# Layer 0's output turned by VectorE and DRAM instead of TensorE, with instruction orders for three engines

## The chip, the core and the metric

The kernel runs on one NeuronCore of a Trainium2 chip. The metric is the device time of one execution in microseconds (us), the median of several runs. A profile of one more execution shows when each instruction ran on the five engines: TensorE (PE in the profile; its weight loads are PEld), VectorE (DVE), ScalarE (ACT), GpSimd (POOL) and SyncE (SP), which here only issues DMA transfers. Each engine works through its own instructions in a fixed order and waits at an instruction whose inputs or buffers are not ready.

## What is computed

The input x has 128 batches of 64 nodes with 256 features. Four graph layers follow each other, each in the form `x = layernorm(x + layer(x))`. The change concerns layers 0 and 1, which the kernel runs in one fused stage:

```python
# layer 0: dense attention over the 64 nodes of a batch
Wh = einsum('bnf,fo->bno', h, W)
e = (Wh @ a1)[:, :, None] + (Wh @ a2)[:, None, :]
e = where(e >= 0, e, 0.2 * e);  e = where(adj == 0, -inf, e)
out = einsum('bij,bjo->bio', softmax(e), Wh)
# layer 1: attention over 512 edges, 4 heads
Xq, Xv = H @ W_lin.T, H @ W_val.T
e = einsum('behd,hd->beh', leaky_relu(Xq[:, src] + Xq[:, dst], 0.2), a) + log(A0[src, dst] + eps)
attn = segment_softmax(e, src)
out = segment_sum(attn[..., None] * Xv[:, dst], src) @ W_out.T
```

Layer 2 (two matrix products with batch norms) and layer 3 (two graph convolutions and four small LSTMs) come after it and are not touched.

## The kernel before

**Quarters.** The fused stage cuts the input into 16 quarters q of 512 rows, that is 8 batches; a batch is called a graph b, 0 to 7. All work is in 32-bit floats. A quarter lives in a tile of 128 partitions by 1024 numbers, `A[:, q]`; before its layer-0 result arrives there, that place is free and serves as scratch.

**Steps of layer 0**, by function: `l0_a` makes the transposed input x^T. For q = 0 TensorE does it (eight 128x128 transposes, ScalarE copies them out). For q ≥ 1 the DMA brings x in "squares": `load_x` issues eight transfers of 64 KB (L135) that put each 32x32 block where it belongs in the transposed layout, and one VectorE instruction (L220, `nc.vector.transpose`) turns every block in itself. `l0_b` multiplies with W (L230) and ScalarE copies the results out; `l0_c` builds the attention logits (transposes L241, VectorE L244 to L248, ScalarE exponentials L251); `l0_d` transposes the attention (L260); `l0_e` multiplies it with Wh (L270), adds x on VectorE (L273), takes mean and variance (L92, L93, L82, L95) and normalises on GpSimd: a power (L83) and four multiply-adds (L97). The result x1 of the quarter goes to `A[:, q]`.

**Steps of layer 1.** `l1_t` transposes x1 on TensorE (L204, eight matmuls) with two ScalarE copies (L205). `l1_qv(q, c2)` makes half of a quarter's queries and values (L295, L298; ScalarE L305, VectorE L306 for the queries' two parts); it is called twice per quarter. `l1_graph(q, b)` is one graph: two matmuls into `z` (L332) and a ScalarE ReLU `u` (L334). `sums` reduces four graphs over the heads (L323). Once for two quarters, in the even quarters, the softmax over edges runs: `l1_softmax` (matmul L342, VectorE scans L344 to L351, ScalarE exponential L352), `l1_sums` (two scans, L357 and L358), `l1_weights` (transposes L366, VectorE L372 and L374, four indirect DMAs to a DRAM table L378 on GpSimd, two loads `ld` from it, L384 on SP). `v_a` copies a quarter's attention out of `ld` on GpSimd (L391) and multiplies it with the values (L399, ScalarE copies L403); `v_b` multiplies with W_out (L413), adds x1 (L415), normalises on VectorE and GpSimd (L97 again, on `y`) and stores the result; `v_c` applies layer 2's adjacency (L433, ScalarE L437).

**Order.** Quarter q's loop runs its eight graphs, and behind each graph the steps of a table `between[b]`, which belong to neighbouring quarters: layer 0 is two quarters ahead, `v_a` three behind (LAG), `v_b` and `v_c` four. The first quarters therefore have no `v` steps and the last two no layer-0 steps. The program is recorded in this order and a scheduler then places every instruction in its engine's queue. `step` ties each step with `tc.issue_after` to the last instruction of the step before; only TensorE's instructions are tied this way. On the other engines the scheduler chose the order. It also chose which of the three PSUM banks named `m` each product takes; a product can only start when the bank's last reader is done.

```python
            if queue:
                with tc.issue_after(queue[-1]):
                    do(n, *more)
            else:
                do(n, *more)
            mine = [t for t in traced[first:] if t.engine == mybir.EngineType.PE]
            queue.extend(mine[-1:])
```

All the transfers of SP go through one queue, in order: loads of x and its squares, the stores of layer 1's result (L418) and the table loads.

## Time and profile before

| | |
|---|---|
| median of 3 runs | 2137.66 us (2136.54 to 2138.21) |
| the profiled execution | 2138.25 us |
| its span in the profile | 2136.4 us |
| TensorE busy | 2060.7 us, 96% of the span |
| ScalarE, VectorE, GpSimd busy | 932.1, 885.9, 430.1 us |
| fused stage (layers 0 and 1) | 0 to about 523 us |
| mean TensorE clock granted | 0.987 |

The profile is read in three steps: which engine is busy nearly all the time and where it is not (busy times by stretch), what it waits for at those places (the timeline with the releaser of each gap), and what the releaser itself was doing before (its own timeline). Busy times of matmuls overlap a little, since they are pipelined; the chain of work that ended last gives lengths without the overlap. The chain lies on TensorE for 86% of the span.

### The profile page before, as it was taken

How to read it: one execution, taken by the hardware profiler on the slowest of the kernel's cores; microseconds unless marked ns; L12 is line 12 of the kernel's file. 1: busy time of each engine (PE TensorE's matmuls, PEld its weight loads, DVE VectorE, ACT ScalarE, POOL GpSimd, SP SyncE). 2: the span in 40 equal slices, each digit the busy share in tenths (PEclk: the TensorE clock that was granted, in tenths of full speed). 3: DMA queues.
4: the chain of work that ended last, by engine and by line, in shares of the span. 5: the costliest groups of instructions: out<-in, count | busy, mean ns of one | idle time of the engine just before them, and what ended most of it. 6: DMA issues, size and time to landing. Idle time of an engine off the chain costs nothing.

```text
span 2136.4 us, 29441 instructions
## 1 busy us (share of the span) xinstructions
PE 2060.7 (96%) x11343; PEld 1330.1 (62%) x11343; DVE 885.9 (41%) x2069; ACT 932.1 (44%) x1795; POOL 430.1 (20%) x569
## 2 busy tenths in 40 slices
PE   5999999998999989999999999999999999999998
PEld 4666767665544444585576576577467468468467
DVE  7456566654444343333234334324324324323213
ACT  2776666664339014334234334334334334333333
POOL 1134334332210010121112112113103103102012
PEclk8999999998999989999999999999999999999999
DMA  5244532322240021012112102103103102101001
GB/s 144 63 69 73 85 61 53 52 43 43 43 118 29 0 89 60 21 54 66 40 46 74 40 29 90 40 11 99 50 6 104 50 1 89 50 1 60 20 1 60
DMA packets 232636, 113.41 MB, mean 53 GB/s; under 512 B 150192, under 2 KB 215728, under 8 KB 232240
## 3 DMA queue, kind: packets, MB, share of 16 engines
q1 hardware_dynamic: 230640, 109.57, 20.2%
q8 instruction: 89, 1.46, 0.3%
q0 software_dynamic: 1024, 1.05, 0.2%
q10 hardware_dynamic: 832, 0.92, 0.1%
q14 instruction: 51, 0.42, 0.1%
HBM read 67.45 MB, written 44.04 MB: 52 GB/s over the span
## 4 chain that ended last, share of the span: by engine, by line
PE 86%; DVE 6%; ACT 4%; issue 2%; POOL 1%; DMA 1%; SPq 0%; POOLq 0%; DVEq 0%; ACTq 0%
PE l L994 36%; PE l L1000 20%; PE pz L784 5%; PE pz L719 5%; PE e L323 3%; PE g L933 2%; PE g L945 2%; PE m L295 2%; PE m L230 2%; PE z L332 2%; PE m L298 2%; PE g L878 1%; PE m L413 1%; PE m L270 1%; ACT u L334 1%
## 5 line engine op out<-in xcount | busy, mean ns | idle before, releaser
L994 PE MATMUL l<-H,wih 128*128 128x256 f32 (+2 forms) x2496 | 787.5, 470 | 1.8 <-ACT H L957 1.2
L994 PEld LDWEIGHTS l<-H,wih 128*128 128x128 f32 x2496 | 471.4, 190 | 286.2 <-issue 185.6
L1000 PE MATMUL l<-hid,whh 128*128 128x256 f32 (+2 forms) x1536 | 435.9, 437 | 0.0
L1000 PEld LDWEIGHTS l<-hid,whh 128*128 128x128 f32 x1536 | 291.8, 190 | 128.4 <-issue 61.2
L1006 ACT ACTIVATE gate_i<-l,bias 128x256 f32<-128x256 f32 (+2 forms) x176 | 100.3, 570 | 441.9 <-PE l L1000 374.2
L1010 POOL TENSOR_TENSOR cell<-gate_f,cell 128x256 f32<-128x256 f32 (+2 forms) x96 | 85.0, 885 | 726.0 <-ACT gate_f L1006 726.0
L1009 DVE TENSOR_TENSOR gate_i<-gate_i,gate_g 128x256 f32<-128x256 f32 (+2 forms) x96 | 49.6, 517 | 415.1 <-ACT gate_g L1006 415.0
L83 POOL TENSOR_TENSOR ln_rs<-ln_rs,mhalf 128x2 f32<-128x2 f32 (+2 forms) x97 | 82.0, 846 | 571.6 <-DVE ln_rs L95 570.7
L334 ACT ACTIVATE u<-z 128x1024 f32<-128x1024 f32 x128 | 130.3, 1025 | 63.3 <-PE z L332 62.3
L1006 ACT ACTIVATE gate_g<-l,bias 128x256 f32<-128x256 f32 (+2 forms) x176 | 100.3, 570 | 107.9 <-PE l L994 59.5
L1014 ACT ACTIVATE gate_g<-cell 128x256 f32<-128x256 f32 (+2 forms) x176 | 90.0, 511 | 86.9 <-DVE cell L1013 45.0
L1013 DVE TENSOR_TENSOR cell<-gate_i,gate_g 128x512 f32<-128x512 f32 (+2 forms) x80 | 48.2, 602 | 186.5 <-ACT gate_g L1006 186.4
L1006 ACT ACTIVATE gate_o<-l,bias 128x256 f32<-128x256 f32 (+2 forms) x176 | 99.3, 564 | 59.9 <-PE l L1000 54.0
L719 PE MATMUL pz<-A,w 128*128 128x512 f32 x256 | 113.1, 595 | 0.0
L332 PE MATMUL z<-gath_r,qs 128*128 128x512 f32 x256 | 100.4, 480 | 0.7 <-ACT u L334 0.4
L306 DVE TENSOR_TENSOR qs<-m,qs 64x256 fp32r<-64x256 f32 x128 | 54.0, 422 | 107.0 <-ACT qs L305 104.8
L719 PEld LDWEIGHTS pz<-A,w 128*128 128x128 f32 x256 | 47.9, 190 | 55.3 <-issue 53.3
L295 PE MATMUL m<-wq,tT 128*128 128x260 f32 x256 | 71.8, 403 | 7.8 <-ACT yT L403 5.4
L1006 ACT ACTIVATE gate_f<-l,bias 128x256 f32<-128x256 f32 (+2 forms) x96 | 51.1, 532 | 59.6 <-PE l L1000 59.1
L1023 DVE TENSOR_TENSOR hid<-gate_o,gate_g 128x256 f32<-128x256 f32 (+2 forms) x96 | 47.4, 493 | 61.2 <-ACT gate_o L1006 35.1
L721 DVE BATCH_NORM_STATS2 st<-pz 128x6 f32<-128x512 f32 x64 | 44.4, 697 | 59.5 <-PE pz L719 59.4
L1023 DVE TENSOR_TENSOR H<-gate_o,gate_g 128x512 f32<-128x512 f32 (+1 forms) x64 | 41.3, 645 | 66.6 <-PE l L994 46.1
(242 smaller groups left out, 2525.2 us busy)
## 6 DMA issues: line engine op xcount, KB each, us to landing
way<-st SPq DMA_DIRECT2D x59, 256.0 KB
st<-way SPq DMA_DIRECT2D x236, 64.0 KB
xin<-in_x SPq DMA_DIRECT2D x16, 512.0 KB
ld<-table SPq DMA_DIRECT2D x16, 512.0 KB
x_dram<-y SPq DMA_DIRECT2D x16, 512.0 KB
x2r<-x_dram SPq DMA_DIRECT2D x32, 256.0 KB
x_dram<-A SPq DMA_DIRECT2D x64, 128.0 KB
x3r<-x_dram SPq DMA_DIRECT2D x64, 128.0 KB
```

Source lines behind the costliest of these rows:

```text
L83: nc.gpsimd.tensor_tensor(dst, dst, mhalf[:, :n], OP.pow)
L295: nc.tensor.matmul(pq, xT[:, k, c * P:(c + 1) * P], wq[:, k, :], start=k == 0, stop=k == KD - 1)
L332: nc.tensor.matmul(z[:, k, :], L1[q]["qs"][c][:, s, k * P:(k + 1) * P], gath_r, start=True, stop=True)
L334: nc.scalar.activation(u, z, AF.Relu)
L719: nc.tensor.matmul(p_, w1[:, k, m * P:(m + 1) * P], A[:, q, k * QT:(k + 1) * QT], start=k == 0, stop=k == KD - 1)
L784: nc.tensor.matmul(p_, w2[:, k, m * P:(m + 1) * P], hidden(q, k), start=k == 0, stop=k == M1 - 1)
L994: nc.tensor.matmul(gates[n], wih[p][:, k, mw * P:(mw + 1) * P], Hw[:, k, :, s, :], start=k == 0, stop=not s and k == KD - 1)
L1000: nc.tensor.matmul(gates[n], whh[p][:, k, m * P:(m + 1) * P], hid[:, k], start=False, stop=k == KD - 1)
L1006: nc.scalar.activation(act[n], gates[n], AF.Tanh if n == "g" else AF.Sigmoid, bias=bias[:, p - 1, m:m + 1])
L1010: nc.gpsimd.tensor_tensor(cell[:, j], act["f"], cell[:, j], OP.mult)
L1014: nc.scalar.activation(act["g"], cell[:, j], AF.Tanh)
L1023: nc.vector.tensor_mul(Hw[:, jj, :, s, :] if over else new[:, jj], o, t)
```

## The change

It has four parts.

First, layer 0's output x1 is no longer transposed by TensorE for q ≥ 2 (`TURN = 2`). `l0_e` stores x1 to DRAM, loads it back in squares with the same eight transfers that x uses (`load_squares`), into the unused place `A[:, q + 1]` (or a free input tile for the last two quarters), and `l1_t` turns the blocks with one VectorE instruction. Quarter 1's input, in turn, is now transposed by TensorE and not by squares. `l0_a` turns x's squares into the next quarter's place; the squares of quarter q+1 are loaded at the end of `l0_b(q)`.

Second, `step` gives orders for TensorE, VectorE and GpSimd: each step's instructions on these engines come behind the last ones of the steps before.

Third, some work gets a step of its own: `v_am` is the GpSimd copy of the attention, cut from `v_a`; `l1_exp` is the softmax's exponential, put behind the last ScalarE instruction recorded; the reciprocal of layer 0's sums moves from `l0_c` to `l0_e`.

Fourth, the table `between` is new. `v_b` and `v_am` stand behind graphs 2 and 3, `v_a` behind graph 5, the queries' first half behind graph 6 and their second half behind graph 0 of the next quarter, `l0_e` behind graph 7.

```diff
+        def load_squares(to, rows):
+            rows = rows.rearrange("(j t) (k i f) -> i k t j f", t=32, k=KD, f=32)
+            for n in range(4):
+                for k in range(KD):
+                    part = to[n * 32:(n + 1) * 32, k * QT:(k + 1) * QT]
+                    nc.sync.dma_start(part.rearrange("t (j f) -> t j f", f=32), rows[n, k])
+        def load_xT(q):
+            load_squares(A[:, q, :], i["x"][q * QT:(q + 1) * QT, :])
...
         def l0_a(q):
             L0[q] = {"x": xin.pop(q)}
-            if q:
-                L0[q]["xT"] = work.tile([P, KD, QT], F32, name="tT", bufs=1)
-                nc.vector.transpose(L0[q]["xT"].rearrange("p k t -> p (k t)"), A[:, q, :])
-            else:
+            if q < TURN:
                 L0[q]["xT"] = transposed(L0[q]["x"], q)
+                return
+            t = A[:, q + 1, :] if q + 1 < NQ else work.tile([P, KD * QT], F32, name="tT", bufs=1)
+            nc.vector.transpose(t, A[:, q, :])
...
             layernorm(token_major(q), x, PQ, nc.gpsimd)
             L0.pop(q)
+            if q >= TURN:
+                x1 = dram.tile([QT, D], F32, name="x1_dram", bufs=2)
+                nc.sync.dma_start(x1.rearrange("(c p) d -> p c d", p=P), token_major(q))
+                sq[q] = A[:, q + 1, :] if q + 2 < NQ else xp.tile([P, PQ, D], F32, name="xin").rearrange(
+                    "p c d -> p (c d)")
+                load_squares(sq[q], x1)
...
+            xT = work.tile([P, KD, QT], F32, name="tT", bufs=1)
+            nc.vector.transpose(xT.rearrange("p k t -> p (k t)"), sq.pop(q))
...
-        def v_a(q):
+        def v_am(q):
             S, b = divmod(q, BPS)
-            v = L1[q]["v"]
-            am = vp.tile([P, PQ * HEADS, N], F32, name="am")
+            am = L1[q]["am"] = vp.tile([P, PQ * HEADS, N], F32, name="am")
             nc.gpsimd.tensor_copy(am.rearrange("p (e r) n -> p e r n", e=2),
                                   ld[S].rearrange("p n (e b r) -> p b e r n", e=2, b=BPS)[:, b])
+        def v_a(q):
+            v, am = L1[q]["v"], L1[q]["am"]
...
-            if queue:
-                with tc.issue_after(queue[-1]):
-                    do(n, *more)
-            else:
+            with ExitStack() as order:
+                for t in latest.values():
+                    order.enter_context(tc.issue_after(t))
                 do(n, *more)
-            mine = [t for t in traced[first:] if t.engine == mybir.EngineType.PE]
-            queue.extend(mine[-1:])
+            for t in traced[first:]:
+                if t.engine in (mybir.EngineType.PE, mybir.EngineType.DVE, mybir.EngineType.Pool):
+                    latest[t.engine] = t
...
-                [(l0_e, q + 1), (l0_a, q + 2)],
-                [(sums, q if q else -1), (l1_softmax, S)],
-                [(l1_sums, S), (l0_b, q + 2)],
-                [(v_b, q - LAG - 1)],
-                [(l1_weights, S), (l1_t, q + 1), (l0_c, q + 2)],
-                [(sums, q), (l1_qv, q + 1, 0)],
-                [(v_c, q - LAG - 1), (v_a, q - LAG)],
-                [(l0_d, q + 2), (l1_qv, q + 1, 1)],
+                [(l0_e, -1 if q else 1), (l0_a, -1 if q else 2), (l1_qv, q if q else -1, 1)],
+                [(sums, q if q else -1), (l1_softmax, S), (l0_b, q + 2), (l1_exp, S)],
+                [(l1_sums, S), (v_b, q - LAG - 1)],
+                [(l0_c, q + 2), (l1_t, -1 if q else 1), (v_am, q - LAG)],
+                [(l1_t, q + 1 if q else -1), (l1_weights, S)],
+                [(sums, q), (v_a, q - LAG)],
+                [(l0_d, q + 2), (l1_qv, q + 1, 0)],
+                [(v_c, q - LAG - 1), (l0_a, q + 3 if q + 4 < NQ else -1), (l0_e, q + 2),
+                 (l0_a, q + 3 if q + 4 == NQ else -1)],
```

## The prediction

> **What bounds the kernel now.** I read the page's busy table first, then the busy times by stretch.

> ```profile
> PE 2060.7 (96%) x11343; PEld 1330.1 (62%) x11343; DVE 885.9 (41%) x2069; ACT 932.1 (44%) x1795; POOL 430.1 (20%) x569
> ...
> 0.00:100.00 100.00, 74.15 (x333) 53.73 (x334) 62.08 (x184) 50.16 (x118) 16.86 (x33) 0.93 0.42 108
> ...
> 300.00:400.00 100.00, 95.45 (x935) 70.06 (x939) 58.68 (x157) 67.52 (x156) 39.59 (x46) 1.00 0.35 62
> ```

> TensorE is the limit. The change touches only the fused stage, 0 to about 523 us (16 quarters q). Its steady part is not far from full: in 300 to 400 us (columns: length, PE, weight load, VectorE, ScalarE, GpSimd, clock, DMA) TensorE is busy 95.45 of 100. So a gain must come from removed matmuls or the few gaps, and a new wait of TensorE costs its full length. The timeline of TensorE shows both kinds:

> ```profile
> 325.53 3.61 PE L413 MATMUL m<-wout,yT 128*128 128x256 f32 x16
> 328.80 0.82 PE L332 MATMUL z<-gath_r,qs 128*128 128x512 f32 x2
> 329.45 1.04 PE L204 MATMUL m<-ident,A 128*128 128x128 f32 x8
> ...
> 338.30 1.25 PE L399 MATMUL m<-am,v 64*64 64x64 f32 x64
> ...
> 360.52 0.79 PE L204 MATMUL m<-ident,A 128*128 128x128 f32 x4 [0.67 <-issue]
> 362.00 0.65 PE L204 MATMUL m<-ident,A 128*128 128x128 f32 x4 [0.69 <-ACT tT L205]
> 362.99 0.66 PE L241 MATMUL m<-ident,sb 128*128 128x128 f32 x4 [0.33 <-DVE ln_mv L93]
> ```

> Two quarters repeat every 61.25 us: the even one, with the softmax, ran 283.46 to 316.23 (32.8), the odd one to 344.72 (28.5). The layer-1 transposes (L204) take 0.87 us in the chain that ended last, plus 0.67 + 0.69 + 0.33 of gaps in even quarters.

> The third view is GpSimd's timeline in an odd quarter:

> ```profile
> 331.17 1.02 POOL L83 TENSOR_TENSOR ln_rs<-ln_rs,mhalf 128x4 f32<-128x4 f32 x1 [2.71 <-DVE ln_rs L95]
> 332.30 2.66 POOL L97 TENSOR_SCALAR y<-y,ln_rs 128x256 f32<-128x256 f32 x4
> ...
> 339.66 1.99 POOL L391 COPY am<-ld 128x1024 f32<-128x1024 f32 x1 [4.70 <-PE m L399]
> ```

> From the last L413 matmul (v_b; ends 329.15 in the chain) to the power is 2.02 us, to the end of the normalisation 5.8. The attention copy at 339.66 is for the *next* quarter's v_a (L399 at 371.01): 29 us early. Here lies the kernel's slack.

> [...](the last but two number of a row is the clock, 1.00 then 0.50):

> ```profile
> 479.00:480.00 1.00, 0.00 (x0) 0.00 (x0) 1.00 (x3) 0.06 (x1) 0.00 (x0) 1.00 0.00 0
> 480.00:481.00 1.00, 0.00 (x0) 0.01 (x1) 1.00 (x2) 0.00 (x0) 0.00 (x0) 1.00 0.00 0
> 481.00:482.00 1.00, 0.98 (x5) 1.00 (x6) 1.00 (x4) 0.00 (x0) 0.00 (x0) 0.50 0.00 0
> ```

> A gap of 2.25 us was enough, and the clock stayed at 0.50 to 487.6. [...]four L97 take 2.17 us at 365.82 but 4.25 at 351.68 beside VectorE's scans. [...]Here a 512 KB store issued at 306.77 moved data until about 310.1, 3.3 us.

> **The change part by part.**

> *Removed.* For q≥2, l1_t's eight matmuls and two ScalarE copies. Per pair 2×0.87 = 1.74 us of TensorE and up to 1.69 of gaps. The copies (4×0.6 per pair) are hidden: ScalarE is busy 67 of 100.

> *Added: the turn through DRAM.* A store, eight loads of 64 KB, one VectorE transpose (1.25 us, L220's row). From quarter start (after l0_e's matmuls): VectorE ends L95 at about 3.2; power 1.1 and L97 2.2 to 4.3 bring x1 to 6.6 to 8.6; store 3.3; eight loads, about 0.6 issue each and 2 to land (274.12 to 281: 6.9). Landed at 17 to 19, turned by 18 to 20. VectorE reaches this transpose at 18.3 in an odd quarter, about 21 in an even one, and l1_qv needs it after 23: hidden, by the stall below. On SP the loads hold up the next quarter's x squares (8×0.6 = 4.8), wanted at about 27 and landed by 24; the table loads stand ahead of the store and issue by 5 us.

> *Quarter 1* goes through TensorE instead of VectorE: eight transposes in the setup, where TensorE waits 2.08 us at 24.95 for VectorE anyway. About −1.5.

> *Orders.* VectorE and GpSimd now keep step order. The exponential behind ScalarE's last, the late reciprocal (0.18) and the queries' halves split over two quarters cost nothing by themselves: total work is the same, and ScalarE reaches the exponential at 12.0 after start, when its input is ready at 11.9. But in the built program's order **every quarter's copy for v_a stands on GpSimd behind the same quarter's v_b normalisation, and v_a on TensorE waits for that copy**. v_a has also moved up from graph 6 to graph 5. Behind v_a on TensorE stand l0_d, the queries' half, v_c and l0_e: everything.

> *Odd quarter.* TensorE to the end of v_b: graph 0.47, half of the queries 3.70, graph 0.47, sums 1.85, l0_b 3.49, graph 0.46, v_b 3.45 = 13.9. Then 2.0 + 1.1 + 2.7 + copy 2.1 = 7.9: copy done at 21.8. TensorE's own work meanwhile is three graphs, l0_c 0.44, sums 1.85 = 3.7, so **it waits 4.2 us**. After: v_a 1.14, graph 0.47, l0_d 0.44, queries 3.9, graph 0.46, v_c 1.14, l0_e 1.73 = 9.3. Sum 31.1 against 28.5: +2.6.

> *Even quarter.* To the softmax's matmul 7.56 (the same with L342's 1.07); scans as at 350.68 to 358.18, 7.5; v_b's VectorE work 3.45 (358.18 to 361.65, without the reciprocal between); 1.1 + 2.7 + 2.1: copy at 24.4. TensorE arrives at 20.2 (7.56 + l0_b 3.49 + v_b 3.45 + four graphs 1.87 + l0_c 0.44 + transposes of the weights 0.87, their second bank about 0.7 late + sums 1.85): waits 4.2. The program also gives v_a's halves one bank (0.65, a ScalarE copy between) and makes the queries wait for the copy of l0_d, behind one u (about 1.4 more). 24.4 + 9.3 + 2.05 = 35.8 against 32.8: +3.0.

> *Clock.* Each 4.2 us wait exceeds the gap that halved the clock. [...]I take 0.7, keeping 0 and 1.7.

> *Pairs.* Quarters 4 to 13: 5×(2.6 + 3.0 + 1.4) = +35. *Early* (no v_b): setup −1.5; quarter 0 about −1.9, half the queries (−3.7) leaving and one l0_e (+1.73) coming; quarter 1, bound by the turn, −1; quarter 2 −3; quarter 3 +3.7, since the first table lands late (ten us from issue to copy, at 316.27 to 326.48) ahead of SP's x1 store. Sum −3.7. *Last two*: v_b, copy, v_a again, and the half of the queries arriving in quarter 15: +3. Sum +34 on the profiled execution's 2138.25 (span 2136.4; the median of the runs, 2137.66, is 0.6 below it): **2172 us**.

> **Rivals.**

> *A: same wait, full clock.* Speaks for it: at 372 to 375 us a gap under 1 us left 1.00. Against: the 2.25 us gap. 5×5.6 − 3.7 + 2 = +26: 2164.

> *B: the turn binds too.* If loads beside the table traffic (DMA share 1.6 for six us at 258 to 264) take ten us as ld's do, and L97 4.3, the transpose ends at 23 to 24, and blocks VectorE's reciprocal and query differences. About 1.5 us more per quarter: 2190. Against: eight loads done in 6.9 at 274.12.

> *C: faster.* v_a's copy is ready when TensorE arrives, so the transposes and their gaps are a clean gain: pair 61.25 − 1.74 − 1.69 = 57.8, five pairs −17, with the early part −21: 2117. Decided at one place: the time from v_b's last matmul to the copy's end must be under 3.7 us. For it: TensorE's removed work is real. Against: the trace's own rows make it 7.9, three of them without variation (power 1.02, copy 1.99).

> *D: a wash.* Fast normalisation (2.2), no bank waits, full clock, and a better early part: pairs +2.5, sum about 0 to +8: 2141.

> That the change doesn't do what it says is excluded by the built order: the transposes are gone for q≥2.

> **How the numbers follow.** Forecast 0.52 (own range 2160 to 2184), A 0.22, B 0.12, C 0.08, D 0.06. Leaving out C, the lower part of D and the top of B gives 2150 to 2192. This kernel's measurement can tell about 0.2%, 4 us. Faster is C, 0.08; within 0.2% most of D, 0.05; slower the rest, 0.87.

> **What would show it.** Right: TensorE's v_a matmuls idle about 4 us before them with GpSimd's copy as releaser, twice per pair; pairs of 66 to 69 us; GpSimd running power, L97, copy without pause; clock below 1.00 after each wait; no wait of any weight on the turning transpose except in quarter 1. Wrong: v_a without a wait (C), or VectorE idle before the transpose on a DMA (B). The weakest terms are the clock and the sum of the early quarters.

## The result, and the profile after

The changed kernel takes **2214.89 us** (median of 4 executions, 2213.13 to 2215.46), the kernel before 2137.1 (2136.41 to 2138.21): a ratio of 1.0362, 95% interval 1.0344 to 1.038. It is 77.8 us slower. The forecast was 2172, its range 2150 to 2192. The forecast had the direction right, and less than half of the size.

The profiled execution took 2215.46 us, with a span of 2213.7 (2136.4 before); the mean clock that TensorE was granted fell from 0.987 to 0.968. The busy table of the page, first row:

```profile
PE 2087.0 (94%) x11239; PEld 1351.7 (61%) x11239; DVE 898.6 (41%) x2082; ACT 921.0 (42%) x1769; POOL 414.4 (19%) x569
```

TensorE does fewer matmuls than before (11239 records in place of 11343) and yet is busy 26 us longer: it worked slower, at a lower clock. Busy times by stretch, columns as in the prediction (length, PE, weight load, VectorE, ScalarE, GpSimd, clock, DMA):

```profile
0.00:100.00 100.00, 72.91 (x321) 51.95 (x321) 60.81 (x181) 48.27 (x110) 16.79 (x33) 0.91 0.40 105
300.00:400.00 100.00, 86.97 (x757) 64.93 (x750) 53.71 (x129) 56.03 (x129) 29.04 (x37) 0.91 0.42 87
```

In the steady part TensorE is now idle for 13 of 100 us (4.5 before), and what it does runs at a mean clock of 0.91.

The waits of TensorE in the first 600 us, largest first (total, times, longest):

```profile
PE m L431 <- POOL am L420: 46.5, 13, 3.9
PE m L321 <- DVE tT L310: 8.6, 3, 4.2
...
PE m L321 <- ACT eT L273: 4.8, 6, 1.1
...
PE m L431 <- ACT yT L435: 4.2, 6, 0.7
PE m L241 <- DVE A L232: 3.9, 1, 3.9
```

Lines have moved: L431 is `v_a`'s matmul, L420 its copy on GpSimd, L310 `l1_t`'s transpose on VectorE, L321 and L324 the queries and values, L358 the graph's z, L349 the sums, L271 and L273 `l0_d`, L283 `l0_e`, L241 `l0_b`, L232 `l0_a`'s transpose, L396 `l1_weights`, L445 and L447 `v_b`, L465 `v_c`. The forecast's main mechanism is there: `v_a` waits for GpSimd 13 times, 3.6 us on average. GpSimd's timeline in the even quarter that starts at 315.10 us shows why (start, length):

```profile
333.64 1.01 POOL L83 TENSOR_TENSOR ln_rs<-ln_rs,mhalf 128x4 f32<-128x4 f32 x1 [11.93 <-DVE ln_rs L95]
334.75 2.66 POOL L97 TENSOR_SCALAR y<-y,ln_rs 128x256 f32<-128x256 f32 x4
337.36 1.89 POOL L420 COPY am<-ld 128x1024 f32<-128x1024 f32 x1
```

The engine was idle for 11.93 us ahead of the normalisation, and the copy, whose input had been loaded long before (issued by 281.7), stands behind it. TensorE's timeline of the same quarter shows the second half of the matter:

```profile
333.46 1.92 PE L349 MATMUL e<-u,apad 128*32 128x512 f32 x16
339.31 1.97 PE L431 MATMUL m<-am,v 64*64 64x64 f32 x32 [3.93 <-POOL am L420]
341.98 1.97 PE L431 MATMUL m<-am,v 64*64 64x64 f32 x32 [0.70 <-ACT yT L435]
343.88 1.22 PE L358 MATMUL z<-gath_r,qs 128*128 128x512 f32 x2
...
346.70 2.10 PE L321 MATMUL m<-wq,tT 128*128 128x260 f32 x4 [0.75 <-ACT eT L273]
```

After the wait each half of `v_a` takes 1.97 us (1.15 at full clock, in an experiment below) and four L321 take 2.10 (1.04 at full clock). The clock was at half from 339.28 to 349.52; four L321 at 350.35 take 1.04 us again.

Where the 77 us of span arose, by quarter (from its first L358, L332 before, to the next quarter's first):

| | before | after | change | forecast |
|---|---|---|---|---|
| up to quarter 0 | 52.89 | 48.27 | −4.6 | −1.5 |
| quarter 0 | 28.78 | 36.04 | +7.3 | −1.9 |
| quarter 1 | 24.99 | 24.14 | −0.9 | −1 |
| quarter 2 | 29.59 | 27.02 | −2.6 | −3 |
| quarter 3 | 24.70 | 34.00 | +9.3 | +3.7 |
| quarters 4, 6, 8, 10, 12 (even) | 32.8 each | 39.9 to 41.3 | +38.2 | +18.5 |
| quarters 5, 7, 9, 11 (odd) | 28.5 each | 32.3 to 32.4 | +15.5 | +13.2 |
| quarter 13 | 28.49 | 38.03 | +9.5 | +3.3 |
| quarters 14 and 15 | 55.48 | 61.57 | +6.1 | +3 |
| all behind | 1613.6 | 1613.2 | −0.5 | 0 |

(The forecast's 3.0 and 2.6 per quarter are given with its 0.7 for the clock.) Three single quarters (0, 3 and 13) and the even ones hold nearly all of the error.

### The profile page after: what moved, and what is told of

Same layout as the page of the kernel before. It is cut to its first block, busy times and chain, and to the rows that moved or that the text cites. A ratio compares the mean times of both kernels' runs of the same rounds, so it can differ in the third digit from the quotient of the medians.

```text
span 2213.7 us, 29494 instructions
## 1 busy us (share of the span) xinstructions
PE 2087.0 (94%) x11239; PEld 1351.7 (61%) x11239; DVE 898.6 (41%) x2082; ACT 921.0 (42%) x1769; POOL 414.4 (19%) x569
## 3 DMA queue, kind: packets, MB, share of 16 engines
q0 software_dynamic: 1024, 1.05, 0.2%
## 4 chain that ended last, share of the span: by engine, by line
PE 84%; DVE 5%; POOL 3%; ACT 3%; issue 2%; DMA 2%; SPq 1%; POOLq 0%; DVEq 0%; ACTq 0%
PE l L1030 34%; PE l L1036 19%; PE pz L820 5%; PE pz L753 5%; PE m L321 3%; PE g L969 2%; PE g L981 2%; PE m L324 2%; PE m L241 2%; PE m L431 1%; POOL y L97 1%; PE g L914 1%; PE z L358 1%; SPq L138 1%; PE m L283 1%
## 5 line engine op out<-in xcount | busy, mean ns | idle before, releaser
L83 POOL TENSOR_TENSOR ln_rs<-ln_rs,mhalf 128x2 f32<-128x2 f32 (+2 forms) x97 | 81.3, 838 | 750.1 <-DVE ln_rs L95 749.5
L332 DVE TENSOR_TENSOR qs<-m,qs 64x256 fp32r<-64x256 f32 x128 | 53.7, 422 | 159.2 <-ACT qs L331 158.6
L358 PE MATMUL z<-gath_r,qs 128*128 128x512 f32 x256 | 104.0, 493 | 3.7 <-ACT u L360 3.7
L321 PE MATMUL m<-wq,tT 128*128 128x260 f32 x256 | 79.8, 441 | 16.1 <-DVE tT L310 8.6
L431 PE MATMUL m<-am,v 64*64 64x64 f32 x1024 | 36.1, 266 | 50.7 <-POOL am L420 46.5
L324 PE MATMUL m<-wv,tT 128*128 128x256 f32 x256 | 74.9, 421 | 0.5 <-ACT v L334 0.5
L331 ACT ACTIVATE qs<-m 64x256 fp32r<-64x256 f32 x128 | 48.2, 376 | 60.0 <-PE m L321 59.0
```

Of the source, the lines that this page charges most:

```text
L83: nc.gpsimd.tensor_tensor(dst, dst, mhalf[:, :n], OP.pow)
L321: nc.tensor.matmul(pq, xT[k][c], wq[:, k, :], start=k == 0, stop=k == KD - 1)
L324: nc.tensor.matmul(pv[:, c % 2, :], xT[k][c], wv[:, k, :], start=k == 0, stop=k == KD - 1)
L358: nc.tensor.matmul(z[:, k, :], L1[q]["qs"][c][:, s, k * P:(k + 1) * P], gath_r, start=True, stop=True)
```

## The experiments

Times are medians; the ratio is to the kernel before, which ran beside them. Its median lay between 2136.4 and 2140.1 us from one group of runs to the next, so across groups a difference of some 4 us is left open. Experiments 1 to 4 are one group, 5, 6 and the first of 7 another, the rest of 7 and 8 a third, 9 the last.

### 1. The copy put first

```diff
-                [(l1_sums, S), (v_b, q - LAG - 1)],
-                [(l0_c, q + 2), (l1_t, -1 if q else 1), (v_am, q - LAG)],
+                [(l1_sums, S), (v_am, q - LAG), (v_b, q - LAG - 1)],
+                [(l0_c, q + 2), (l1_t, -1 if q else 1)],
```

> The changed kernel, with GpSimd's copy for v_a put ahead of v_b's normalisation (graph 2) in place of behind it. Theory T (the loss is TensorE's wait for this copy, and the half clock that follows the wait): no wait of weight on the copy from quarter 4 on; TensorE arrives at v_a 20.3 us after the start of an even quarter and 18.4 of an odd one, and what is behind takes 10.7 and 9.3 us at full clock, so even quarters 31 and odd ones 27.7 (39.9 and 32.3 now, 32.8 and 28.5 in the kernel before); quarters 0, 3 and 13 keep their losses, the turn's wait in quarter 13 grows to about 8 us. About 2140 us (2132 to 2148). Rival R (the turn through DRAM or the fixed orders are the cause, and the wait only moves on to the next late thing, the turned output): pairs stay at 68 to 72 us, 2195 to 2215.

Measured: 2160.28 us, 1.0099 (1.0082 to 1.0115): 54.6 us of the 77.8 are gone by moving one instruction of GpSimd, though the time is 12 us over the expected range. Odd quarters take 27.9 us, as theory T had it (27.7), less than before the change. Quarter 13's wait went as well, where 8 us had been expected: SP now issued the loads for the turn ahead of layer 1's store. But even quarters take 33.9 to 38.7 where 31 was expected. TensorE's timeline in the even quarter that starts at 235.41:

```profile
255.62 1.15 PE L431 MATMUL m<-am,v 64*64 64x64 f32 x32
258.63 1.15 PE L431 MATMUL m<-am,v 64*64 64x64 f32 x32 [1.86 <-ACT yT L435]
259.70 0.74 PE L358 MATMUL z<-gath_r,qs 128*128 128x512 f32 x2
...
262.24 2.10 PE L321 MATMUL m<-wq,tT 128*128 128x260 f32 x4 [0.69 <-ACT eT L273]
```

`v_a` starts without a wait, but its second half waits for ScalarE's copy of the first: both halves have the same PSUM bank. ScalarE comes to that copy (L435) only behind four exponentials:

```profile
257.62 0.39 ACT L264 ACTIVATE e<-e,mx 128x128 f32<-128x128 f32 x1
257.91 0.18 ACT L264 ACTIVATION_READ_ACCUMULATOR e<-e,mx 128x1 f32 x1
258.00 0.57 ACT L435 ACTIVATE yT<-m 128x512 f32<-128x512 f32 x1
```

And the clock was at half for 6.8 us from 260.55, though no wait in this quarter was longer than 1.86 us.

### 2. TensorE kept busy during the wait

The wait stays, but TensorE multiplies something in it (the results are overwritten by `v_a` itself).

```diff
             pY = [bank([KD, PQ, N]) for _ in range(2)]
+            for _ in range(8 if q + LAG < NQ else 0):
+                nc.tensor.matmul(pY[0].rearrange("p k c n -> p (k c n)"), L1[q + LAG]["qs"][2][:, 0, :P], gath_r,
+                                 start=True, stop=True)
```

> The changed kernel with eight more matmuls of z's shape (128x512, 0.40 us each, 3.2 us) ahead of v_a on TensorE, whose results are overwritten: TensorE works in place of waiting, and the copy comes as late as before. Theory T: the wait before v_a falls under 1 us, the copy still ends 24.2 and 21.9 us after the start, the clock stays 1.00 behind it, and the clock's share of the loss goes: even quarters from 39.9 to about 35.2 us, odd ones from 32.3 to 31.2; with quarters 13 and 14 about 2183 us (2176 to 2192). Rival R2 (v_a's matmuls and what is behind are slow for another reason, the shared PSUM bank and the waits for ScalarE, not for the clock): at most 3 us, 2212 to 2218.

Measured: 2196.99 us, 1.0266 (1.0249 to 1.0283): 17.9 us faster than the changed kernel by *more* work. The expected 2183 was missed, because eight such matmuls took 2.0 us and not 3.2: a wait of 1.9 us was left in even quarters, and half-speed windows of 3.4 to 6.8 us with it. In odd quarters (wait left 1.51 us) the clock held, and they fell from 32.3 to 30.85. Rival R2 (not the clock) is out; the size is settled in experiment 9.

### 3. `v_a` later

```diff
-                [(sums, q), (v_a, q - LAG)],
-                [(l0_d, q + 2), (l1_qv, q + 1, 0)],
+                [(sums, q)],
+                [(l0_d, q + 2), (l1_qv, q + 1, 0), (v_a, q - LAG)],
```

> The changed kernel with v_a alone moved to graph 6, behind l0_d and the first half of the next queries, as in the kernel before; GpSimd's order is untouched, and the copy still stands behind v_b. Theory T: TensorE now has 4.6 us more of other work before v_a and arrives 23.4 (odd) and 25.5 us (even) after the start, when the copy is done (21.9 and 24.2): no wait, full clock, the same as with the copy put first but for 3 us: 2137 to 2148. Rival R (turn or orders): unchanged, 2205 to 2215.

Measured: 2181.06 us, 1.0193 (1.0176 to 1.021). The wait for the copy is gone as expected, but the time is 33 us over the range. TensorE now comes earlier to `l0_d`, and waits there for ScalarE's exponentials: 1.49 us in each odd quarter, and in even ones 0.64 and then 1.05 for L273. The clock halved for 3.4 us in every quarter from 4 to 12, with no longer wait than these in it. Theory T was too narrow: `v_a`'s wait is the first of several that stand one behind the other.

### 4. The turn undone

```diff
-            if q < TURN:
+            if q < NQ:
                 xT = transposed(token_major(q))
...
-            if q >= TURN:
+            if q >= NQ:
                 x1 = dram.tile([QT, D], F32, name="x1_dram", bufs=2)
```

> The changed kernel with layer 0's output of every quarter turned by TensorE again (eight transposes and two ScalarE copies, no store, no loads); orders and table of calls as changed. Theory T: 0.87 us of transposes per quarter fall into the wait for the copy, which shrinks to about 3.0 (even) and 2.6 us (odd), and the quarter ends as late; the turn's own waits in quarters 3 and 13 (4.1 and 4.2 us, with the half clock after them) go: 2195 to 2208, or 15 us less if the shorter waits no longer halve the clock. Rival R (the turn is the cause): under 2160. Rival S (the removed transposes are a real gain of 1.74 us and more per pair, now given back): 2225 to 2235.

Measured: 2169.47 us, 1.0149 (1.0132 to 1.0166), between theory T's lower case (2180) and rival R (2160). Giving TensorE its eight transposes per quarter back saves 45 us. Of these, 9.0 us come in quarter 3 and 7.2 in quarter 13, whose waits for the turn are gone, as theory T had it. The odd quarters end 1.5 us earlier: the copy still comes at 21.9 us after the start, and the wait of 3.16 us (3.52 in the changed kernel) halved the clock in one of five only. In even quarters (33.8 to 37.4 us) the wait fell to 2.6, and `v_a`'s halves got two banks, so that the wait inside it is gone.

### 5. Copy first and turn undone

Edits 1 and 4 together:

```diff
-                [(l1_sums, S), (v_b, q - LAG - 1)],
+                [(l1_sums, S), (v_am, q - LAG), (v_b, q - LAG - 1)],
...
-            if q < TURN:
+            if q < NQ:
                 xT = transposed(token_major(q))
```

> The kernel with the copy put first, and layer 0's output turned by TensorE again. Theory T: there is no wait of TensorE left in odd quarters to hide the transposes, so an odd quarter grows from 27.9 to about 28.9 us; even quarters stay at 34 to 38; quarter 3 gains 8 us (no wait for the turn): 2155 to 2168 us. Rival R (the turn costs in every quarter): under 2145.

Measured: 2130.81 us, **0.9974 (0.9968 to 0.9981): faster than the kernel before**, and far under the 2155 expected. From experiment 1 to this one an odd quarter grows by only 0.4 us (27.9 to 28.4 on average), so the transposes that the change removed were worth less than half of their 0.87 us. Even quarters shrink from 36.5 to 31.9 on average; part of that is the wait inside `v_a` (1.86 us in experiment 1, now 0.49 for VectorE's L402), since the scheduler gave its halves two banks here. Quarter 3 falls from 32.7 to 24.8. No half-speed window is left in quarters 4 to 13 (81.9 us of them in the changed kernel, 30.7 in experiment 1). So the turn, with what followed from it, cost much more than it saved. Rival R, as worded (under 2145), is what the run shows.

### 6. Orders undone, and orders alone

Changed kernel with orders for TensorE only:

```diff
-                if t.engine in (mybir.EngineType.PE, mybir.EngineType.DVE, mybir.EngineType.Pool):
+                if t.engine in (mybir.EngineType.PE,):
```

> The changed kernel with orders for TensorE alone, as before; VectorE's and GpSimd's order is the scheduler's. In the built program two copies for v_a stand together, ahead of the pair's v_b normalisations, and quarter 2's turn stands ahead of the setup's work on VectorE. Theory T: no wait of v_a on the copy, so about the time with the copy put first, 2160, less quarter 0's wait for the turn on VectorE (3.9 us and its half clock, together about 7): 2145 to 2160. Rival (the waits are the table's, whatever the order on GpSimd): 2200 to 2215.

Measured: 2159.79 us, 1.0115 (1.0098 to 1.0132): at the upper end of the expectation. The scheduler put two copies together once in two quarters: even quarters (32.7 us) have no wait for them, odd ones (32.2) still 3.35 us. Even ones now wait 1.41 us for the turned output (L310). Quarter 0 fell to 29.8.

Kernel before with the changed `step`, its table and transposes as they were:

```diff
-            mine = [t for t in traced[first:] if t.engine == mybir.EngineType.PE]
-            queue.extend(mine[-1:])
+            for t in traced[first:]:
+                if t.engine in (mybir.EngineType.PE, mybir.EngineType.DVE, mybir.EngineType.Pool):
+                    latest[t.engine] = t
```

> The kernel before with the orders for VectorE and GpSimd alone; its table and TensorE's transposes stay. The copy now stands on GpSimd behind the same quarter's v_b, about 22 (odd) and 24 us (even) after the start, and v_a stays at graph 6, where TensorE comes to it at 22 to 26 us. Theory T (the copy behind v_b costs because v_a also comes early): waits under 1 us, 2137 to 2150. Rival (the orders are harmful by themselves): over 2165.

Measured: 2206.57 us, 1.0327 (1.031 to 1.0345). The expectation was badly wrong: orders alone cost 70 us, 45 of them in the five even quarters from 4 to 12, 9 in quarter 14 and 7 in quarter 0. In this table `v_a`, with the copy in it, comes behind `l1_weights`, and with GpSimd's order kept the copy also stands behind that step's four indirect DMAs. GpSimd and TensorE in the even quarter that starts at 314.55:

```profile
335.29 1.09 POOL L378 DMA_INDIRECT table<-at,place  x1 [0.17 <-DVE e L244]
338.80 0.96 POOL L378 DMA_INDIRECT table<-at,place  x1 [2.42 <-DMA table<-at,place]
341.68 0.96 POOL L378 DMA_INDIRECT table<-at,place  x1 [1.93 <-DVE qs L306]
344.56 0.96 POOL L378 DMA_INDIRECT table<-at,place  x1 [1.92 <-DMA table<-at,place]
345.52 1.90 POOL L391 COPY am<-ld 128x1024 f32<-128x1024 f32 x1
```

```profile
347.48 1.99 PE L399 MATMUL m<-am,v 64*64 64x64 f32 x64 [5.93 <-POOL am L391]
```

The second and the fourth DMA wait for the landing of the one before (for the third, after a gap of the same length, the profile names VectorE), so the copy came 33 us after the start. The changed table, with the copy as a step of its own ahead of `l1_weights`, avoids this; it stops one step short, behind `v_b`.

### 7. What is left in even quarters

Experiment 1 with `v_a` moved up to graph 4, ahead of `l1_weights`, whose two row tiles hold two banks:

```diff
-                [(l1_t, q + 1 if q else -1), (l1_weights, S)],
-                [(sums, q), (v_a, q - LAG)],
+                [(l1_t, q + 1 if q else -1), (v_a, q - LAG), (l1_weights, S)],
+                [(sums, q)],
```

> The kernel with the copy put first (first experiment), and v_a moved up once more, to graph 4, ahead of the softmax's transposes (l1_weights). What is left in even quarters of the first experiment is 33.9 us where the clock held and 36 to 39 where it did not, against 31 expected. Theory B (l1_weights takes two of the three PSUM banks until VectorE's L404, so v_a's halves share the third, and the second half waits 1.86 us for ScalarE, which also halves the clock): the wait inside v_a goes, the clock stays, even quarters 31.5 to 33 us, odd ones stay at 27.9: 2160 - 5 x 4.5 = about 2138 us (2130 to 2146). Rival C (ScalarE's exponentials and the first queries' copy are late anyway, and TensorE waits for them in place of v_a): even quarters 35 to 37, 2152 to 2162.

Measured: 2160.36 us, 1.0116 (1.0099 to 1.0133), no gain. Even quarters fell to 32.2 to 33.9 us, as theory B had it: the wait inside `v_a` is gone. But odd ones rose from 27.9 to between 28.3 and 32.2, because TensorE came earlier to the queries and waited there, in quarters 5, 7 and 9 for 1.3 to 2.0 us for the turned output (L310).

Experiment 1 with `v_a` writing to one of z's double banks:

```diff
+            both = bank([2, E], name="z", bufs=2)
+            pY = [both[:, s, :].rearrange("p (k c n) -> p k c n", k=KD, c=PQ) for s in range(2)]
```

> The kernel with the copy put first, and v_a's two halves written to one of z's double banks in place of two m banks. Theory B (in even quarters the second half of v_a waits 1.86 us because both halves share the one m bank that l1_weights leaves, and the wait halves the clock): the wait inside v_a goes, even quarters fall from 36 to 39 to 32 to 33.5 us, odd ones stay at 27.9: 2140 us (2134 to 2148). Rival C (ScalarE is late for what follows in any case, and TensorE only waits a little later): 2153 to 2162.

Measured: 2157.63 us, 1.0101 (1.0077 to 1.0125), within noise of experiment 1. Again the bank was the cause inside `v_a`: even quarters took 32.0 to 33.9 us. Again the wait went on: to L321, 2.03 us for L273 in even quarters, and for the turned output in odd ones (3.07 us in quarter 5). Theory B was right on the place and wrong on the gain.

### 8. Repaired with the turn, and without it

Experiment 5 with quarter 0's order changed:

```diff
-                [(l0_e, -1 if q else 1), (l0_a, -1 if q else 2), (l1_qv, q if q else -1, 1)],
+                [(l0_a, -1 if q else 2), (l0_e, -1 if q else 1), (l1_qv, q if q else -1, 1)],
```

> The kernel with the copy put first and TensorE turning, and in quarter 0 VectorE's transpose for quarter 2 (L232) put ahead of layer 0's end of quarter 1 in place of behind it. Theory: the 3.9 us wait of l0_b for it and the half clock behind it go, quarter 0 falls from 36.1 to about 29 us: 2124 us (2120 to 2128). Rival (the squares' load or something else in quarter 0 is late anyway): 2129 to 2133.

Measured: 2127.39 us, 0.9942 (0.9924 to 0.996): 3.4 us less than experiment 5 by the medians, 6.8 by the ratios to the kernel before beside each; expected were 7. Quarter 0 fell from 36.1 to 31.4 us and what leads up to it by 3.4, so the edit gained 8.1 us there; even quarters then took 0.7 to 1.2 us longer, with no half-speed window, and why stays open.

The same, with `v_a` in z's double bank:

> As the second of these four, with v_a in z's double bank. Theory B: where TensorE turns, v_a's halves already have two banks (even quarters 31.7 us with a wait of 0.5 us for VectorE's L402 left), so little is gained: 2119 to 2126 us. Rival (a double bank of z held by v_a delays the graphs, whose z then waits for ScalarE): 2127 to 2140.

Measured: **2121.0 us, 0.992 (0.9904 to 0.9937), the fastest of all,** and in theory B's range. In the profiled execution, the shortest of this kernel's (2116.42 us), even quarters take 30.5 us (quarter 4 32.1) and odd ones 28.2; TensorE is busy 98.9 of 100:

```profile
300.00:400.00 100.00, 98.91 (x868) 73.19 (x867) 61.17 (x161) 68.97 (x155) 37.31 (x45) 1.00 0.46 77
```

The edit is that of experiment 7's second kernel. And with the turn through DRAM kept from quarter 5 on, all else as in that kernel:

```diff
-            if q < NQ:
+            if q < 5:
                 xT = transposed(token_major(q))
...
-            if q >= NQ:
+            if q >= 5:
```

> The turn through DRAM kept from quarter 5 on, with everything that the runs blame taken away: copy first, v_a in z's banks, quarter 0 as in the run beside it, quarters 2 to 4 turned by TensorE. Theory (the turn itself is a gain of about 0.9 us a quarter once no wait takes it back): even quarters 32 to 33, odd ones 27.9, quarter 3 25: 2119 to 2128 us. Rival (the transposes were work that fell into waits anyway): not under the run with TensorE turning, 2124 to 2135.

Measured: 2133.75 us, 0.9981 (0.9972 to 0.999): 12.8 us slower than with TensorE turning, so moving the turn away from TensorE is the loss here, and the theory's range is missed. The profiled execution was the longest of this kernel's (2145.55 us), so its waits are larger than usual. It shows two places. Even quarters mostly take 32.0 us (30.5 with TensorE turning): from quarter 6 on TensorE waits at the queries 2.03 us for ScalarE's L273. Odd ones take 29.0 to 36.1 us and wait for the turned output, 4.07 us in the longest, which starts at 315.98 (TensorE; then VectorE):

```profile
336.62 1.48 PE L271 MATMUL m<-ident,e 128*128 128x128 f32 x4
342.17 1.24 PE L321 MATMUL m<-wq,tT 128*128 128x260 f32 x2 [4.07 <-DVE tT L310]
```

```profile
340.88 1.25 DVE L310 STREAM_TRANSPOSE tT<-A 128x1024 f32<-128x1024 f32 x1 [4.84 <-DMA A<-in_x]
```

The way through SP that made it late:

```profile
322.39 3.24 SPq L414 DMA_DIRECT2D ld<-table  x2
325.73 4.10 SPq L293 DMA_DIRECT2D x_dram<-A  x1
...
333.69 5.03 SPq L138 DMA_DIRECT2D A<-x_dram  x8
```

(The transpose's releaser is named as a load of x, issued on the same queue; its own loads are those of the last row.) x1 is ready 7.7 us after the quarter's start. Behind two table loads its store is issued at 9.8, and its issue lasts 4.10 us (0.38 in the quarter that starts at 315.10 in the changed kernel; why is not shown). The loads go at 17.7, and the turned output is there at 26.2; TensorE wants it at about 22. In the changed kernel the table loads are issued 4.0 us before an odd quarter starts (350.94); here the even quarters end sooner, and the same loads fall 6.4 us into the odd one, ahead of the store. So this wait is one that the slower kernel did not have. A turn whose store does not stand behind the table loads was not tried.

### 9. The size of the error

Sixteen in place of eight matmuls ahead of `v_a`:

```diff
-            for _ in range(8 if q + LAG < NQ else 0):
+            for _ in range(16 if q + LAG < NQ else 0):
```

> The changed kernel with sixteen in place of eight extra matmuls ahead of v_a (eight took 2.0 us of the 3.9 us wait, so sixteen cover about 4.0). Theory T: the clock stays 1.00 through the even quarter, which then ends where the forecast had it without the clock, 35.1 to 35.8 us, an odd one 31.2 (the extra work now overshoots by 0.5): pairs of 66.4 to 67 in place of 72 to 73, in all 2183 us (2177 to 2190). Rival (the two short waits behind v_a, 0.7 us each, hold the clock down even without the long one): even quarters stay at 37, 2190 to 2197.

Measured: 2185.16 us, 1.0222 (1.0205 to 1.0239), as theory T had it. TensorE's timeline in the even quarter that starts at 235.80, where L427 are the extra matmuls and L434 `v_a`:

```profile
256.00 4.02 PE L427 MATMUL m<-gath_r,qs 128*128 128x512 f32 x16
260.17 1.15 PE L434 MATMUL m<-am,v 64*64 64x64 f32 x32 [0.15 <-POOL am L420]
262.02 1.15 PE L434 MATMUL m<-am,v 64*64 64x64 f32 x32 [0.70 <-ACT yT L438]
```

The copy comes as late as before (24.2 us), but even quarters now take 35.05 us in three of five and 36.7 in two with one half-speed window, odd ones 31.15. Half-speed time in quarters 4 to 13 fell from 81.9 to 13.7 us.

The changed kernel without the three single waits: quarter 0's order as in experiment 8, and quarters 4 and 14 turned by TensorE:

```diff
-            if q < TURN:
+            if q < TURN or q in (4, 14):
                 xT = transposed(token_major(q))
...
-            if q >= TURN:
+            if q >= TURN and q not in (4, 14):
```

> The changed kernel without the three single waits that the forecast did not have: VectorE's turn for quarter 2 ahead of layer 0's end of quarter 1, and quarters 4 and 14 turned by TensorE; copy and v_a as changed. Theory T: quarter 0 falls from 36.0 to about 31, quarter 3 from 34.0 to 25, quarter 13 from 38.0 to 32.3, the pairs stay at 72 to 73: 2195 us (2188 to 2201). Rival (these waits only take up time that the waits of v_a would take anyway): 2205 to 2215.

Measured: 2196.12 us, 1.0275 (1.0258 to 1.0293), in theory T's range: quarter 0 31.0 us, quarter 13 32.3; the even quarters stay at 39.9 to 41.5. Quarter 3 took 28.2 where 25 was expected: a wait of 2.63 us for the copy is left in it.

Both:

> Both edits of the two runs beside it. If the clock and the three single waits are all that the forecast lacked, this kernel's time is about the forecast's: 2163 us (2155 to 2172). If something else is missing, the two gains do not add up: over 2175.

Measured: 2166.22 us, 1.0134 (1.0117 to 1.0151). The gains over the changed kernel are 29.7 and 18.8 us, together 48.5; both at once give 48.7. The quarters agree with the forecast one by one too: odd ones 31.15 (31.1 without the clock), even ones 35.05 to 36.8 (35.8). The early sum is −4.0 (−3.7), but that is luck: setup −6.8 for −1.5 and quarter 0 +2.7 for −1.9 make up for each other.

## Why the prediction was right and wrong

**Right: the direction and the main mechanism.** In the changed kernel the copy's end was forecast at 21.8 and 24.4 us after the quarter's start and came at 21.9 and 24.2; the wait, forecast at 4.2 us, was 3.5 (odd) and 3.9 (even). The step lengths stood too: with the clock kept, odd quarters take 31.15 us (forecast 31.1) and even ones mostly 35.05 (35.8). GpSimd runs power, L97 and copy without a pause, as said. Putting the copy first gives 54.6 us back. Two of its signs failed: pairs took 72 to 74 us (the last 78) in place of 66 to 69, and the turning transpose was waited for not in quarter 1 (0.3 us) but in quarters 3 and 13 (4.1 and 4.2). It had named the clock and the sum of the early quarters as its weakest terms, and these are the two that failed, with quarter 13.

**Wrong: the clock, "I take 0.7, keeping 0 and 1.7".** This term was 7 us for ten quarters; filling the wait, which takes it away, gave 29.7 in all, 28.2 of it in these ten. All three numbers were the author's estimate. The most that it kept, 1.7, is half of 3.41 us, and 3.41 us is what the four odd quarters show: the clock was at half once in each, for that long (376.83 to 380.24 in one of them). In the five even ones it stayed at half for 10.2 to 13.7 us. Busy times of the changed kernel in windows of 3.41 us, laid close to the recorded changes of the clock (even quarter, then odd):

```profile
335.93:339.34 3.41, 0.03 (x2) 0.03 (x2) 3.38 (x6) 1.65 (x8) 3.33 (x4) 0.99 0.32 130
339.34:342.75 3.41, 2.71 (x46) 2.53 (x48) 0.45 (x3) 0.60 (x1) 1.33 (x2) 0.50 0.10 34
342.75:346.17 3.42, 3.20 (x30) 2.34 (x26) 0.00 (x0) 1.63 (x3) 1.50 (x2) 0.50 0.06 14
346.17:349.58 3.41, 2.88 (x7) 2.32 (x8) 0.34 (x1) 0.85 (x2) 1.00 (x2) 0.51 0.04 10
```

```profile
373.47:376.88 3.41, 0.02 (x3) 0.02 (x3) 1.34 (x2) 1.65 (x8) 3.34 (x4) 0.99 0.55 163
376.88:380.30 3.42, 3.42 (x69) 3.00 (x70) 0.00 (x0) 1.35 (x3) 0.00 (x0) 0.51 0.09 31
380.30:383.71 3.41, 3.41 (x18) 3.01 (x17) 0.84 (x2) 2.40 (x7) 0.00 (x0) 1.00 0.00 0
```

In both, an empty window (0.03, 0.02 of 3.41) is followed by half speed (0.50, the third number from the end; 0.99 and 0.51 come from the rows' edges, which lie 0.05 to 0.06 us behind the changes). The odd quarter fills the next window (3.42 of 3.42), and the clock is back. In the even one the next windows have the two short waits that the forecast itself had found (0.70 at 341.98 inside `v_a`, 0.75 at 346.70 before the queries), and the clock stays down. They were priced at their own length; behind the long wait they went with a clock that stayed at half. That they keep it there is read from this comparison and from the counts at the end; no run takes away these two waits alone.

The kernel before had shown as much, in the one place that the forecast used. Half speed lasted there from 481.00 to 487.82 (the forecast read 487.6), two windows, with a second wait in the first of them:

```profile
481.02 1.09 PE L366 MATMUL m<-ident,dn 128*128 128x128 f32 x4 [2.25 <-DVE dn L358]
481.90 1.06 PE L204 MATMUL m<-ident,A 128*128 128x128 f32 x4
483.65 1.11 PE L204 MATMUL m<-ident,A 128*128 128x128 f32 x4 [0.69 <-ACT tT L205]
```

Half of 6.8 us is 3.4, twice the most that the forecast kept.

**Wrong: the early quarters, "Sum −3.7"; it was +8.5.** Up to quarter 0 and in quarters 1 and 2 the forecast was near or too cautious. Quarter 0 was summed from the work that leaves and comes (−1.9), and the order of VectorE was left out. VectorE's and TensorE's timelines in the changed kernel:

```profile
58.86 0.16 DVE L95 TENSOR_SCALAR ln_rs<-ln_mv 128x4 f32<-128x4 f32 x1
59.16 1.25 DVE L232 STREAM_TRANSPOSE A<-A 128x1024 f32<-128x1024 f32 x1
```

```profile
60.55 5.86 PE L241 MATMUL m<-w,A 128*128 128x258 f32 x13 [3.91 <-DVE A L232]
```

The transpose for quarter 2, which needs nothing of quarter 1, stands behind quarter 1's statistics, only because its step is written behind them; TensorE waits 3.91 us, with 6.8 us at half speed from 59.39 on. Quarter 3 had its reason in the forecast (the first table ahead of SP's store of x1), with 3.7 us; it was 9.3: `v_a` waits 3.12 for the late table and the queries then 4.08 for the turn, each with 3.41 us at half speed behind (from 154.96 and from 161.79).

**Wrong: quarter 13, priced like every odd one.** The turn of quarter 14 falls into this quarter, and its loads go to a tile of `xin`. SP's timeline:

```profile
507.47 0.39 SPq L293 DMA_DIRECT2D x_dram<-A  x1
520.94 0.34 SPq L450 DMA_DIRECT2D x_dram<-y  x1
521.37 5.65 SPq L138 DMA_DIRECT2D xin<-x_dram  x8
```

The loads stand behind layer 1's store (L450), which waits for `v_b`'s normalisation: 14 us after the store of x1. TensorE waits 4.23 us for L310. In experiment 1, where SP issues the loads ahead of that store, the wait is gone. The forecast had counted what the loads hold up on SP, not what holds up the loads here. These three quarters (0, 3 and 13) together are worth 18.8 us.

**The rivals.** A, the same wait at full clock, had 2164; the kernel with that clock and without the single waits takes 2166. C's condition (v_b's last matmul to the copy's end under 3.7 us) was not met: 7.6 us in the odd quarter that starts at 354.96. B (the turn binds too) had a chance of 0.12. In the changed kernel it binds in two quarters only, since the turned output is there at 19.8 us in an odd quarter and 22.2 in an even one, before TensorE comes out of `v_a`'s wait. Once that wait is taken away it binds in odd quarters (experiments 7 and 8). The forecast took "hidden, by the stall below" as an end of the matter, and rival C counted the removed transposes as a gain of up to 1.74 us and 1.69 of gaps per pair. Measured with the stall gone, from experiment 5 to 1, their removal gains 0.4 per odd quarter and loses 4.6 in an even one; with all else repaired (experiment 8) it loses 12.8 us in all.

## What to carry to other kernels

When an engine gets a fixed order, list for each of its instructions what now stands ahead of it and was not needed: one copy behind a normalisation that it does not use cost 55 us, one transpose behind another quarter's statistics 3 to 8, and where the same copy stood behind four indirect DMAs, orders alone cost 70. Price a wait of TensorE by its length and by the windows behind it: in the changed kernel half speed lasted 3.41 us in the odd quarters 5 to 11, where no such wait followed, and 10.2 to 13.7 us in the even ones, where two short waits followed (in the one above, 0.70 and 0.75 us within 7.5 us of 339.28). And a wait that a bigger wait hides has to be priced again for the day when the bigger one is gone. Matmuls that fill such gaps need not be a cost: eight transposes per quarter, and even sixteen useless matmuls, made the changed kernel faster (2169.5 and 2185.2 us in place of 2214.9).

## What the runs showed of the hardware

| TensorE busy in a window | at full clock: next window at half | at half: next window at half |
|---|---|---|
| under 40% | 106 of 106 | 13 of 13 |
| 40 to 60% | 40 of 99 | 19 of 19 |
| 60 to 80% | 12 of 278 | 49 of 49 |
| 80 to 90% | 0 of 235 | 6 of 24 |
| over 90% | 0 of 1916 | 8 of 148 |

So in these traces the clock fell behind every window under 40% (106), behind fewer than half of those at 40 to 60% (40 of 99), and behind none of the 2151 over 80%; once down, it came back only behind windows over 80% (158 of 172). The kernel before and the changed one alone show the same: under 40% it fell behind 3 of 3 and 15 of 15 windows, over 80% behind none of 136 and none of 101. A wait of the same length did not always halve it: that of 3.16 us in experiment 4 did in one odd quarter of five. This is a count, not a test of its own. Windows laid 0.1 us to either side move some counts into a neighbouring row. Of the windows at half in the even quarter above, one that was 94% busy did not bring the clock back and one at 84% did, so the border is not sharp.
